# Layer 0's cross-attention by halves of eight tiles, with block transposes on VectorE and row-tiled sums on TensorE

## The chip, the core and the metric

One core of a Trainium2 chip runs the whole computation in one launch. The metric is the device time of that launch in microseconds, the median of a few runs. TensorE multiplies matrices into PSUM (eight banks of 128 partitions x 512 fp32), VectorE and ScalarE work on PSUM and SBUF, GpSimd on SBUF, and SyncE issues most of the DMAs. All data are fp32.

## The reference

Two layers follow each other. Layer 0 has one head: 2048 states x of width 256 attend to 1601 context tokens of width 192, and a gate mixes the result into the state. Layer 1 has 16 heads of width 16: self-attention over the 2048 states, cross-attention over the context, and an MLP. The change is in layer 0, whose reference is:

```python
tok = input_tokens @ W_proj + b_proj
scores = jnp.einsum('bnd,bsd->bns', prev_states, tok) / jnp.sqrt(jnp.float32(D))
attn = jax.nn.softmax(scores, axis=-1)
routed = jnp.einsum('bns,bsd->bnd', attn, tok)
ps_n = _ln(prev_states, g_state, beta_state)
in_n = _ln(routed, g_input, beta_input)
...
return _ln(new_state, g_out, beta_out)
```

Both kernels never form tok. They project the query instead (y = x W_proj^T, so that a score is y times the context token, plus x times b_proj), sum the context tokens under the probabilities (the mean context, width 192), and project that mean by W_proj.

## The kernel before

The 2048 states are 16 tiles of 128. The context lies transposed in two buffers: ctxA holds its first 128 features, ctxB the last 64, twice, on partitions 0 to 63 and 64 to 127. `queries` (L233) makes y for 512 states at a time. For a tile, `scores_a` (L252) multiplies the 128 features and `scores_b` (L266) the 64 features, key pieces alternating between the two copies of ctxB, which use different 64-row groups of the array; the scores of 1601 keys fill one PSUM tile of four banks, of which there is one. `scores_b` also forms the bias x times b_proj (L279, L281), takes the maximum (L283 to L285) and the exponential with its sum (L288), and the sum's reciprocal (L292).

`l0_values` (L321) transposes the probabilities on TensorE, 13 blocks of up to 128 keys (L327), copies them out of PSUM (L331, L333, L336), multiplies them by the context with keys on partitions (`ctxn`, L339, 13 matmuls of 192 columns), and scales by the reciprocal (L347). `l0_turn` (L350) transposes that mean context (2 transposes, L353, and a copy, L357); `l0_project` (L360) multiplies by W_proj (L362), adds b_proj (L365) and takes the statistics of the result and of x (`norm_stats`, L148: L150 and L151).

The loop at L404 runs these functions one tile apart: scores of tile t, the turn and projection of tile t-2, the values of tile t-1. Within layer 0 nothing is pinned: a scheduler places the instructions of each engine by priority and readiness. After tiles 6, 10 and 14, `begin_in` (L373) starts the inverse roots of the variances for four tiles (`inverse_root`, L153: two steps on VectorE, twelve on GpSimd, L166 to L169, then `ms` on VectorE, L379), and `normed_tile` and `routed_tile` normalize four tiles (L388, L394). Loads stand on SyncE's queue in the order of L92 to L207, the weights of the gate and of layer 1 among them.

`l0.close()` (L420) frees the PSUM banks, and all later work takes its banks from a new pool of eight. From there on every instruction is pinned in program order (`kept`, `mm` at L432, `transpose` at L435). What comes first is written out by hand as a list of steps, FIRST (L1018: ti are transposes of the normalized inputs, u, r, c the gate's matmuls, bi the inverse roots, nx and nr normalizations, and so on); then the attention of layer 1 runs from about 405 us, its 32 x 128 score matmuls on four row groups at once.

Of the kernel before, what the change touches and what calls it, by code (L numbers as in the profile page):

```python
# [70 lines left out]
def xattn_kernel(  # L71
# [19 lines left out]
    w_proj_sb = pa.tile([CK, 2, D], F32, name="w_proj_sb")  # L91
    nc.sync.dma_start(w_proj_sb, w_proj.rearrange("(c p) n -> p c n", p=CK))  # L92
    xT_sb = pa.tile([P, 2, S], F32, name="xT_sb")

    def load_xT(b):
        at_b = slice(b * QB, (b + 1) * QB)
        nc.sync.dma_start(xT_sb[:, :, at_b], xT.rearrange("(c p) n -> p c n", p=P)[:, :, at_b])
# [3 lines left out]

    ctxA = pa.tile([P, L], F32, name="ctxA")
    nc.sync.dma_start(ctxA, ctxT[:P])
    ctxB = pa.tile([P, L], F32, name="ctxB")
# [3 lines left out]
    nc.scalar.dma_start(cols_sb, cols)  # L108

# [24 lines left out]
    def load_compact(pool, w, p, name, queue=nc.gpsimd):  # L134

        k, n = w.shape
        stage = w_prep.tile([p, k // p, n], F32, name="stage")
        queue.dma_start(stage, w.rearrange("(c p) n -> p c n", p=p))
        t = pool.tile([p, k // p, D], F32, name=name)
        for c in range(k // p):  # L140
            nc.gpsimd.tensor_copy(
                t[:, c, :].rearrange("p (h w) -> p h w", w=HD),
                stage[:, c, :].rearrange("p (h w) -> p h w", w=HP)[:, :, :HD],
            )
        return t


    def norm_stats(mv, src, t):  # L148
        st = small.tile([P, 6], F32, name="bn_st", bufs=4)
        nc.vector.bn_stats(st, src)  # L150
        nc.vector.bn_aggr(mv[:, t, :], st)  # L151

    def inverse_root(var, name, n=4, bufs=2, keep=None):  # L153


        keep = keep or kept
        v, y, a = (small.tile([P, n], F32, name=f"{name}_{x}", bufs=bufs) for x in "vya")
        i32 = mybir.dt.int32
        keep(nc.vector.tensor_scalar_add(v, var, EPS))
        keep(  # L160
# [4 lines left out]
        for _ in range(3):  # L165
            keep(nc.gpsimd.tensor_mul(a, y, y))  # L166
            keep(nc.gpsimd.tensor_mul(a, a, v))
            keep(nc.gpsimd.tensor_scalar(a, a, -0.5, 1.5, ALU.mult, ALU.add))
            keep(nc.gpsimd.tensor_mul(y, y, a))  # L169
# [12 lines left out]
    pw = l0.enter_context(tc.tile_pool(name="pw", bufs=2, side="right"))  # L182
    y_sb = pa.tile([P, 2, S], F32, name="y_sb")
    ctxn = pa.tile([P, len(LC), C], F32, name="ctxn")
# [8 lines left out]
    nc.sync.dma_start(l0_rows, rows[:first_rows].partition_broadcast(P))  # L193
    load_x(0)
    load_xT(1)
    load_xT(2)
    load_xT(3)
    for t4 in range(1, 4):
        load_x(t4)
    w_u_sb = load_weights(p0, w_u, P, "w_u_sb", nc.sync)  # L200
    w_r_sb = load_weights(p0, w_r, P, "w_r_sb", nc.sync)
    w_n_sb = load_weights(p0, w_n, P, "w_n_sb", nc.sync)
    nc.sync.dma_start(rows_sb, rows[first_rows:].partition_broadcast(P))
    sa_wk_sb = load_compact(w_prep, sa_wk, P, "sa_wk_sb", nc.sync)
    sa_wv_sb = load_compact(w_prep, sa_wv, P, "sa_wv_sb", nc.sync)
    ca_wk_sb = load_compact(w_prep, ca_wk, CK, "ca_wk_sb", nc.sync)
    ca_wv_sb = load_compact(w_prep, ca_wv, CK, "ca_wv_sb", nc.sync)  # L207

    ps_s = l0.enter_context(tc.tile_pool(name="ps_s", bufs=1, space=PSUM))
    ps = tc.alloc_tile_pool(name="ps_tok", bufs=4, space=PSUM)  # L210

    warm = pa.tile([P, QB], F32, name="warm")
    nc.vector.memset(warm, 0.0)
    pt = ps.tile([P, QB], F32, name="tok_ps")
    for _ in range(3):
        nc.tensor.matmul(pt, warm[:, :P], warm, start=True, stop=True)


    wT_sb = pa.tile([P, 2, D], F32, name="wT_sb")
    pt = ps.tile([P, QB], F32, name="tok_ps")  # L220
    for d in range(2):
        for c in range(2):
            nc.tensor.transpose(
                pt[:, d * C + c * CK : d * C + (c + 1) * CK],
                w_proj_sb[:, c, d * P : (d + 1) * P],
                ident[:CK, :CK],
            )
    wT = pt[:, : 2 * C].rearrange("p (d n) -> p d n", d=2)
    nc.vector.tensor_copy(wT_sb[:, :, :C], wT)
    nc.scalar.copy(wT_sb[:, :, C:], wT[:, :, P:])  # L230


    def queries(b):  # L233
        for m in range(2):
            pt = ps.tile([P, QB], F32, name="tok_ps")
            for c in range(2):
                nc.tensor.matmul(  # L237
                    pt,
                    wT_sb[:, c, m * P : (m + 1) * P],
                    xT_sb[:, c, b * QB : (b + 1) * QB],  # L240
# [3 lines left out]
            copy = nc.vector.tensor_copy if m else nc.scalar.copy  # L244
            copy(y_sb[:, m, b * QB : (b + 1) * QB], pt)
# [3 lines left out]
    LEFT = 2 * QB - (L + 1) // 2  # L249
    KEYS = [(0, QB - LEFT), (QB - LEFT, QB), (2 * QB - LEFT, QB), (3 * QB - LEFT, L - 3 * QB + LEFT)]  # L250

    def scores_a(t):  # L252

        sc = ps_s.tile([P, 4 * QB], F32, name="l0_sc")[:, LEFT : LEFT + L]
        for n0, nw in KEYS:
            nc.tensor.matmul(  # L256
                sc[:, n0 : n0 + nw],
                y_sb[:, 0, t * P : (t + 1) * P],
                ctxA[:, n0 : n0 + nw],
# [928 lines left out]
```

## Time and profile before

| what | us |
|---|---|
| median of 3 runs (1946.67 to 1948.96) | 1947.11 |
| the profiled execution, its own time | 1949.57 |
| its span, first to last instruction | 1947.8 |
| outside the span | 1.8 |
| layer 0, up to layer 1's first transposes | 217.0 |
| FIRST, up to the attention loop | 188.0 |
| attention and MLP, to the end | 1542 |
| mean granted TensorE clock | 0.998 |

Over the span TensorE is busy 99% of the time, VectorE 73%, ScalarE 69%, GpSimd 34%. These are averages over stages that differ, so a stage is read from a window: its length, then for each engine the busy time with the count of instructions in brackets, the granted clock, the DMA share and the rate. The chain of waits is followed back from the last instruction; read forward it gives start, duration, engine and line. A group of instructions gives busy time, mean length of one in ns, idle time of its engine ahead of them, and what ended most of that idle time.

### The profile page before, as it was taken

What the parts mean: (1) busy time and instruction counts of PE and PEld (TensorE: products, weight loads), DVE (VectorE), ACT (ScalarE), POOL (GpSimd) and SP (SyncE); (2) the same over time, 40 slices, a digit from 0 to 9 for tenths busy, and PEclk for the clock granted to TensorE, in tenths of its full rate; (3) what the DMA queues carried; (4) which work ended last, traced back from release to release, by engine and by line L of the source; (5) the groups of instructions that cost most, each with busy time, mean ns of one, the idle gap of its engine ahead of it and who ended that gap; (6) DMA issues with size and microseconds to landing.
All of it is one profiled execution on the core that took longest, in us unless ns stands there. A gap on an engine that the chain in (4) does not pass through costs nothing.

```text
span 1947.8 us, 37207 instructions
## 1 busy us (share of the span) xinstructions
PE 1932.9 (99%) x13800; PEld 884.6 (45%) x13800; DVE 1425.3 (73%) x2617; ACT 1342.0 (69%) x2555; POOL 657.9 (34%) x833
## 2 busy tenths in 40 slices
PE   8999999999999999999999999999999999999999
PEld 4778776533333333443333334433333433443366
DVE  3444477778888888888888888788888878886210
ACT  2322433268887888788878887887888788888621
POOL 0100324124443444344344444343544344443010
PEclk9999999999999999999999999999999999999999
DMA  7000402600000000000000000000000000000000
GB/s 227 12 1 1 60 1 56 82 14 5 5 5 5 5 5 5 5 5 8 5 5 5 5 5 5 5 5 4 26 27 5 6 6 5 5 5 2 1 22 22
DMA packets 25605, 33.15 MB, mean 17 GB/s; under 512 B 11984, under 2 KB 17808, under 8 KB 25040
## 3 DMA queue, kind: packets, MB, share of 16 engines
q1 hardware_dynamic: 23200, 24.21, 5.7%
q0 software_dynamic: 1568, 4.90, 0.9%
q10 hardware_dynamic: 656, 1.67, 0.6%
q8 instruction: 108, 1.77, 0.4%
q14 instruction: 73, 0.60, 0.1%
HBM read 16.21 MB, written 2.62 MB: 10 GB/s over the span
## 4 chain that ended last, share of the span: by engine, by line
PE 93%; DVE 5%; POOL 1%; DMA 1%; issue 0%; ACT 0%; SPq 0%; DVEq 0%; ACTq 0%
PE bank L432 82%; PE l_rp L339 3%; PE l_sc L256 2%; DVE mxp L585 2%; PE l_sc L270 1%; PE l_tp L327 1%; PE bank L435 1%; PE l_rp L362 1%; DMA xT_sb<-in_xT_dram 1%; PE tok_ps L237 1%; DVE bn_st L807 0%; DVE bn_st L742 0%; DVE res L908 0%; PE l_rp L353 0%; POOL ca_wo_sb L451 0%
## 5 line engine op out<-in xcount | busy, mean ns | idle before, releaser
L585 DVE TENSOR_REDUCE mxp<-bank 128x1 f32<-128x512 f32 x1792 | 1109.0, 681 | 176.7 <-PE bank L432 170.3
L631 ACT ACTIVATE pt<-bank 128x512 f32<-128x512 f32 (+1 forms) x1856 | 960.2, 603 | 202.7 <-PE bank L432 201.2
L657 POOL TENSOR_TENSOR acc<-acc,part 128x512 f32<-128x512 f32 x414 | 525.1, 1268 | 841.4 <-ACT part L656 841.4
L432 PE MATMUL bank<-qa,k_sa 32*128 32x512 f32 x2048 | 520.0, 615 | 0.4
L432 PE MATMUL bank<-k_sa,qa 32*128 32x512 f32 x2048 | 507.1, 618 | 1.3 <-DVE mxp L585 0.8
L432 PE MATMUL bank<-k_ca,qa 32*128 32x512 f32 (+1 forms) x2048 | 432.9, 532 | 0.0
L432 PE MATMUL bank<-qa,k_ca 32*128 32x512 f32 (+1 forms) x1664 | 414.7, 617 | 0.0
L432 PEld LDWEIGHTS bank<-qa,k_sa 32*128 32x128 f32 x2048 | 215.8, 183 | 226.0 <-DVE mxp L585 203.5
L432 PE MATMUL bank<-pt,v_sa 128*32 128x512 f32 x2048 | 272.8, 605 | 0.4
L656 ACT COPY part<-bank 128x512 f32<-128x512 f32 x414 | 253.0, 611 | 13.5 <-PE bank L432 10.8
L432 PEld LDWEIGHTS bank<-qa,k_ca 32*128 32x128 f32 (+1 forms) x1664 | 166.3, 179 | 179.2 <-DVE mxp L585 143.4
L432 PEld LDWEIGHTS bank<-k_sa,qa 32*128 32x128 f32 x2048 | 199.4, 183 | 71.9 <-ACT pt L631 42.9
L432 PE MATMUL bank<-pt,v_ca 128*32 128x512 f32 (+1 forms) x1664 | 225.0, 605 | 0.3
L432 PEld LDWEIGHTS bank<-k_ca,qa 32*128 32x128 f32 x2048 | 196.9, 184 | 46.6 <-ACT pt L631 31.5
L432 PEld LDWEIGHTS bank<-pt,v_sa 128*32 128x32 f32 x2048 | 40.3, 108 | 192.7 <-ACT pt L631 191.7
L432 PEld LDWEIGHTS bank<-pt,v_ca 128*32 128x32 f32 (+1 forms) x1664 | 34.6, 108 | 151.1 <-ACT pt L631 149.0
L1106 DVE TENSOR_TENSOR o<-bank,res 128x512 f32<-128x512 f32 (+1 forms) x9 | 5.6, 630 | 97.1 <-PE bank L432 97.1
L339 PE MATMUL l_rp<-ctxn,l_pT 128*128 128x192 f32 (+1 forms) x416 | 70.4, 326 | 0.3 <-DVE routed L365 0.3
L283 DVE TENSOR_REDUCE l_nmx<-l_sc 128x1 f32<-128x1601 f32 x16 | 29.2, 1825 | 56.6 <-PE l_sc L270 56.6
L339 PEld LDWEIGHTS l_rp<-ctxn,l_pT 128*128 128x128 f32 (+1 forms) x416 | 67.2, 190 | 0.5 <-DVE routed L365 0.5
L357 ACT COPY l_uT<-l_rp 96x256 f32<-96x256 f32 x16 | 5.9, 367 | 73.9 <-PE l_rp L353 73.9
L432 PE MATMUL bank<-hT_sa,k_sa 128*128 128x512 f32 x128 | 55.7, 593 | 0.0
(189 smaller groups left out, 1393.4 us busy)
## 6 DMA issues: line engine op xcount, KB each, us to landing
xT_sb<-in_xT_dram SPq DMA_DIRECT2D x4, 512.0 KB
res<-in_x_dram SPq DMA_DIRECT2D x4, 512.0 KB
k_sa<-hT_sa SPq DMA_DIRECT2D x16, 128.0 KB
k_sa<-k SPq DMA_DIRECT2D x64, 32.0 KB
qa<-hT_sa SPq DMA_DIRECT2D x64, 32.0 KB
qa<-hT SPq DMA_DIRECT2D x64, 32.0 KB
k_sa<-in_mlp_w_dram POOLq DMA_DIRECT2D x2, 1024.0 KB, 6.1
out_dram<-o SPq DMA_DIRECT2D x7, 256.0 KB
```

Of the source, the lines that this page charges most:

```text
L237: nc.tensor.matmul(pt, wT_sb[:, c, m * P : (m + 1) * P], xT_sb[:, c, b * QB : (b + 1) * QB], start=(c == 0), stop=(c == 1),)
L256: nc.tensor.matmul(sc[:, n0 : n0 + nw], y_sb[:, 0, t * P : (t + 1) * P], ctxA[:, n0 : n0 + nw], start=True, stop=False, skip_group_check=True,
L270: nc.tensor.matmul(sc[:, n0 : n0 + nw], y_sb[r, 1, t * P : (t + 1) * P], ctxB[r, n0 : n0 + nw], start=False, stop=True, skip_group_check=True,
L283: nc.vector.tensor_reduce(nmx, sc, AX.X, ALU.max, negate=True)
L327: nc.tensor.transpose(tp[:kw, i, :], pr[:, k0 : k0 + kw], ident)
L339: nc.tensor.matmul(rp[:, :C], pT[:kw, i, :], ctxn[:kw, i, :], start=(i == 0), stop=(i == len(LC) - 1),)
L362: nc.tensor.matmul(rp[:, :D], uT[:, c, :], w_proj_sb[:, c, :], start=(c == 0), stop=(c == 1))
L432: kept(nc.tensor.matmul(out_, lhsT, rhs, **kw))
L585: kept(nc.vector.tensor_reduce(mxps[n][:, j, qt, kb : kb + 1], mx, AX.X, ALU.max))
L631: kept(nc.scalar.activation(pt[:kw], sc[:kw], AF.Exp, scale=HD**-0.5))
L656: kept(nc.scalar.copy(part, av))
L657: kept(nc.gpsimd.tensor_add(accs[n], accs[n], part))
```

## The change

Layer 0 is rewritten and pinned in program order.

- **PSUM.** One pool of four halves of two banks serves everything in layer 0, in rotation. Scores of a tile take two halves (801 and 800 keys); maximum and exponential run once per half.
- **Bias.** x times b_proj runs on GpSimd, its sum on ScalarE.
- **Transposes.** The probabilities (1601 keys filled up to 1632) are transposed by one VectorE instruction per tile in 32 x 32 blocks, into a buffer that holds eight tiles: on row group i (32 partitions) stand the keys of a block against the states 32i to 32i+31 of each tile.
- **Context.** TensorE transposes the context as before; then 20 SBUF-to-SBUF DMAs on SyncE's queue (16, and 4 for the last key) put each block of 32 keys on all four row groups (ctx4). Their source lies where the transposed probabilities of tiles 6 and 7 go later. The last two loads of x stand behind them.
- **Mean context.** For eight tiles at a time: 51 key blocks x 4 row groups, each a matmul of 32 x 128 with 256 columns (8 tiles x 32 states), and the same for the other 64 features, where key blocks alternate between the two column halves of the array. The four accumulators are all four halves. The result is already transposed; eight copies put it over y's buffer (alternating halves of the 64 features are summed by W_proj's lower part being there twice).
- **Projection.** Eight matmuls of 256 columns for four tiles into one half; the reciprocal and b_proj are applied by one VectorE instruction per tile, with the statistics behind it.
- **Order.** Scores of tiles 0 to 7, the first mean, scores of tiles 8 to 15, projection and inverse roots of the first eight tiles, the second mean, projection of the rest. The statistics of x stand ahead of the first mean. The gate's weights are loaded over the context's buffer after tile 15, and the row constants after them; layer 1's weights pass one by one through one staging buffer. FIRST loses the steps that moved into layer 0 (nx1, bi0, bi1) and gets bi2 and bi3.

```diff
@@ loads and buffers @@
-    w_proj_sb = pa.tile([CK, 2, D], F32, name="w_proj_sb")
-    xT_sb = pa.tile([P, 2, S], F32, name="xT_sb")
-    ctxA = pa.tile([P, L], F32, name="ctxA")
+    w_projA = pa.tile([P, D], F32, name="w_projA")
+    w_projB = pa.tile([P, D], F32, name="w_projB")
+    xy_sb = pa.tile([P, 2, S], F32, name="xy_sb")
+    ctx_w = p0.tile([P, 2 * L], F32, name="ctx_w")
+    ctxA, ctxB = ctx_w[:, :L], ctx_w[:, L:]
...
+    pr_xn = p0.tile([P, 2, LP], F32, name="pr_xn")
+    pT = pa.tile([P, T8, LP], F32, name="l0_pT")
+    ctx4 = pa.tile([P, KB, C], F32, name="ctx4")
+    wT_sb = rows_sb[:, : 2 * D].rearrange("p (d n) -> p d n", d=2)
+    xbs = [rows_sb[:, (2 + i) * D : (3 + i) * D] for i in range(2)]
+    stage = rows_sb[:, 4 * D : 8 * D]
...
-    ps_s = l0.enter_context(tc.tile_pool(name="ps_s", bufs=1, space=PSUM))
-    ps = tc.alloc_tile_pool(name="ps_tok", bufs=4, space=PSUM)
+    halves = l0.enter_context(tc.tile_pool(name="halves", bufs=4, space=PSUM))
+    def half():
+        return halves.tile([P, 2, QB], F32, name="half")
...
@@ scores_a, scores_b, l0_values, l0_turn, l0_project become @@
+    def query_bias(t):
+
+        xb = xbs[t % 2]
+        kept(nc.gpsimd.tensor_mul(xb, res[:, t, :], row("b_proj")))
+        kept(nc.scalar.activation(xb, xb, AF.Identity, accum_out=cbs[:, t : t + 1]))
...
+    def scores(t):
+        hs = [half().rearrange("p b n -> p (b n)") for _ in range(2)]
+        pieces = [hs[0][:, LEFT:], hs[1][:, : L - H0]]
+        outs = [pieces[i // 2][:, n0 - (i // 2) * H0 :][:, :nw] for i, (n0, nw) in enumerate(KEYS)]
+        tok = slice(t * P, (t + 1) * P)
+
+
+        for o, (n0, nw) in zip(outs, KEYS):
+            mm(
+                o, xy_sb[:, 0, tok], ctxA[:, n0 : n0 + nw],
+                start=True, stop=False, skip_group_check=True,
+            )
+        for i, (o, (n0, nw)) in enumerate(zip(outs, KEYS)):
+            r = slice(i % 2 * (C - P), (i % 2 + 1) * (C - P))
+            mm(
+                o, xy_sb[r, 1, tok], ctxB[r, n0 : n0 + nw],
+                start=False, stop=True, skip_group_check=True,
+            )
+        nm2 = small.tile([P, 2], F32, name="l0_nm2")
+        for i in range(2):
+            kept(nc.vector.tensor_reduce(nm2[:, i : i + 1], pieces[i], AX.X, ALU.max, negate=True))
+        nmx = small.tile([P, 1], F32, name="l0_nmx")
+        cb = cbs[:, t : t + 1]
+        kept(
+            nc.vector.scalar_tensor_tensor(
+                nmx, nm2[:, 0:1], nm2[:, 1:2], cb, ALU.min, ALU.subtract
+            )
+        )
+        kept(nc.vector.tensor_scalar(nmx, nmx, cb, 1.0 / 16.0, ALU.add, ALU.mult))
+        for i, (k0, kw) in enumerate(((0, H0), (H0, L - H0))):
+            kept(
+                nc.scalar.activation(
+                    pr_xn[:, t % 2, k0 : k0 + kw], pieces[i], AF.Exp, bias=nmx, scale=1.0 / 16.0,
+                    accum_out=dens[:, t, i : i + 1],
+                )
+            )
+
+    def turned(t):
+        kept(nc.vector.transpose(pT[:, t % T8, :], pr_xn[:, t % 2, :]))
...
+    def spread_context():
+        for j in range(P // HP):
+            r = slice(j * HP, (j + 1) * HP)
+            n = (KB - 1 - j) // 4 + 1 if j != (KB - 1) % 4 else (KB - 1) // 4
+            for i in range(P // HP):
+                nc.sync.dma_start(ctx4[i * HP : (i + 1) * HP, j::4, :][:, :n, :], tok_ctx[r, :n, :])
+        left = L - (KB - 1) * HP
...
+    def mean_context(h):
+
+
+        accs = [half() for _ in range(4)]
+
+        def part(dst, i, kb, feats, **kw):
+            r = slice(i * HP, (i + 1) * HP)
+            mm(
+                dst[:, : T8 * HP].rearrange("p (t a) -> p t a", a=HP),
+                ctx4[r, kb, feats],
+                pT[r, :, kb * HP : (kb + 1) * HP],
+                skip_group_check=True,
+                **kw,
+            )
+
+        for kb in range(KB):
+            for i, acc in enumerate(accs):
+                part(acc[:, 0, :], i, kb, slice(0, P), start=(kb == 0), stop=(kb == KB - 1))
+        for kb in range(KB):
+            c = slice(kb % 2 * (C - P), (kb % 2 + 1) * (C - P))
+            for i, acc in enumerate(accs):
+                part(acc[c, 1, :], i, kb, slice(P, C), start=(kb < 2), stop=(kb >= KB - 2))
...
+        for c in range(2):
+            for i, acc in enumerate(accs):
+                copy = nc.vector.tensor_copy if (i % 2 and c) else nc.scalar.copy
+                kept(
...
+    def project(t4):
+
+        pt = half().rearrange("p b (i d) -> p (b i) d", d=D)
+        for i in range(4):
+            tok = slice((4 * t4 + i) * P, (4 * t4 + i + 1) * P)
+            for c, w in enumerate((w_projA, w_projB)):
+                mm(pt[:, i, :], xy_sb[:, c, tok], w, start=(c == 0), stop=(c == 1))
+        return pt
+
+    def project_end(t4, pt):
+        for i in range(4):
+            t = 4 * t4 + i
+            kept(
+                nc.vector.scalar_tensor_tensor(
+                    routed[:, t, :], pt[:, i, :], rdens[:, t : t + 1], row("b_proj"),
+                    ALU.mult, ALU.add,
+                )
+            )
+            norm_stats(mv_r, routed[:, t, :], t)
...
@@ the order @@
-    pend, mean = (0, *got), None
-    for t in range(1, NT):
-        sc = scores_a(t)
-        if mean:
-            mean = l0_turn(*mean)
-        got = scores_b(t, sc)
-        if mean:
-            l0_project(*mean)
-        mean = l0_values(*pend)
-        pend = (t, *got)
-        if t in (6, 10, 14):
-            begin_in((t - 6) // 4, loose)
-        if 8 <= t < 12:
-            normed_tile(xn0[t - 8], t - 8, loose)
-            routed_tile(t - 8, loose)
-    l0_project(*l0_turn(*mean))
-    l0_project(*l0_turn(*l0_values(*pend)))
+    xns = {b: [pr_xn[:, b, i * D : (i + 1) * D] for i in range(4)] for b in range(2)}
+    xns.update({2: xns[0], 3: xns[1]})
+
+
+    queries(0)
+    query_bias(0)
+    scores(0)
+    turn_context(0, 4)
+    turn_context(4, 4)
+    query_bias(1)
+    scores(1)
+    turned(0)
+    turn_context(8, 4)
+    turn_context(12, 1)
+    spread_context()
+    for t4 in range(2, 4):
+        load_x(t4)
+    queries(1)
+    for t in range(2, T8):
+        query_bias(t)
+        scores(t)
+        turned(t - 1)
+    queries(2)
+    queries(3)
+    turned(T8 - 1)
+    for t in range(T8, NT):
+        query_bias(t)
+    sa_wk_sb = load_compact(w_prep, sa_wk, P, "sa_wk_sb", nc.sync, stage)
+    sa_wv_sb = load_compact(w_prep, sa_wv, P, "sa_wv_sb", nc.sync, stage)
+    wqs = {"sa": load_compact(w_prep, sa_wq, P, "sa_wq_sb", nc.sync, stage)}
+    ca_wk_sb = load_compact(w_prep, ca_wk, CK, "ca_wk_sb", nc.sync, stage)
+    ca_wv_sb = load_compact(w_prep, ca_wv, CK, "ca_wv_sb", nc.sync, stage)
+    for t in range(NT):
+        norm_stats(mv_x, res[:, t, :], t)
+    mean_context(0)
+    scores(T8)
+    for t in range(T8 + 1, NT):
+        scores(t)
+        turned(t - 1)
+
+    w_u_sb, w_r_sb, w_n_sb = (
+        ctx_w[:, i * 4 * D : (i + 1) * 4 * D].rearrange("p (c n) -> p c n", n=D) for i in range(3)
+    )
+    for t, w in ((w_u_sb, w_u), (w_r_sb, w_r), (w_n_sb, w_n)):
+        nc.sync.dma_start(t, w.rearrange("(c p) n -> p c n", p=P))
+    nc.sync.dma_start(rows_sb, rows[first_rows:].partition_broadcast(P))
+    got = [project(t4) for t4 in range(2)]
+    turned(NT - 1)
+    for t4 in range(2):
+        project_end(t4, got[t4])
+        begin_in(t4)
+    for b in range(2):
+        for i in range(4):
+            normed_tile(xns[b][i], 4 * b + i)
+    for t in range(4):
+        routed_tile(t)
+    mean_context(1)
+    got = [(t4, project(t4)) for t4 in range(2, 4)]
+    for t4, pt in got:
+        project_end(t4, pt)
     l0.close()
...
@@ FIRST @@
-        "nx1 ti0.2 ti0.3 ti0.0 ti0.1 ti1.0 bi3 nr2 nr1 ti1.1 u0.0 r0.0 r0.1 u0.1 nx2 c0.0 ti1.2 "
-        "b0.0 ti1.3 nr3 c0.1 b0.1 ro0 r1.0 ti2.0 r1.1 no0.0 ti2.1 u1.0 no0.1 no0.2 no0.3 ti2.2 "
+        "ti0.2 ti0.3 ti0.0 ti0.1 ti1.0 nr1 ti1.1 u0.0 r0.0 bi2 r0.1 u0.1 nx2 c0.0 bi3 ti1.2 "
+        "b0.0 ti1.3 nr2 c0.1 b0.1 nr3 ro0 r1.0 ti2.0 r1.1 no0.0 ti2.1 u1.0 no0.1 no0.2 no0.3 ti2.2 "
```

## The prediction

> **What bounds the kernel now.** I read the clock, the chain that ended last, the chain inside one tile of layer 0, and the windows by stage. The granted clock is 0.998, so durations are full-rate ones. The chain of the whole span, by engine:
>
> ```profile
> PE 93%; DVE 5%; POOL 1%; DMA 1%; issue 0%; ACT 0%; SPq 0%; DVEq 0%; ACTq 0%
> ```
>
> TensorE carries it. Layer 0 is the stretch up to 217 us, where layer 1's first transposes start. One tile of it, in the chain of waits:
>
> ```profile
> 47.84 2.69 PE l_sc L256 x8
> 50.54 0.22 PE l_rp L353 x2
> 50.76 1.54 PE l_sc L270 x8
> 52.30 1.06 PE l_rp L362 x4
> 53.36 1.44 PE l_tp L327 x13
> 54.80 4.25 PE l_rp L339 x26
> ```
>
> Nothing but TensorE: 11.2 us a tile, every one back to back. 4.23 are scores; 1.44 + 4.25 transpose probabilities and sum the context; 0.22 + 1.06 turn and project. The windows (a tile, the last tile, what follows layer 0):
>
> ```profile
> core 0: us, PE busy (x) PEld busy (x) DVE busy (x) ACT busy (x) POOL busy (x), PEclk, DMA share, GB/s
> 35.40:38.90 3.50, 3.50 (x7) 1.88 (x8) 0.56 (x1) 0.31 (x1) 0.73 (x2) 0.52 0.42 126
> 59.06:70.30 11.24, 11.24 (x62) 8.93 (x62) 5.22 (x14) 3.13 (x5) 0.00 (x0) 1.00 0.01 2
> 205.96:217.00 11.04, 9.18 (x53) 7.38 (x52) 3.30 (x11) 1.72 (x4) 0.46 (x1) 1.00 0.00 0
> 217.00:405.00 188.00, 186.20 (x779) 118.41 (x780) 131.75 (x291) 61.98 (x101) 54.68 (x170) 0.99 0.35 54
> 405.00:1947.00 1542.00, 1538.46 (x11978) 611.14 (x11976) 1202.24 (x2078) 1222.47 (x2361) 586.76 (x576) 1.00 0.03 7
> ```
>
> VectorE (5.22) and ScalarE (3.13) leave half of a tile free, so work can be moved to them. What TensorE saves before 217 us moves all that follows forward; the last two rows, 1730 us, are untouched but for a few reordered instructions.
>
> **The rates.** An fp32 matmul is two passes of the array, and the scores' first eight passes (2 x 1601 columns) take 2.69 us: 0.84 ns a column, 0.427 us for 512, 0.2135 for 256. Thirty-two-row tiles on four row groups run side by side: in layer 1, 16 passes of 512 columns take 1.93 us (1001.16 to 1003.09), 3.5 times faster than 16 x 0.427, and inside the burst four passes start every 0.429, so the full factor of 4 once running. Four 32-column tiles with 128 rows also run together (8 passes, L432 pt,v_sa, in about 1.0 us). Row and column tiles at once are not in the trace.
>
> **Scores.** TensorE does the same 2.69 + 1.54 = 4.23. What VectorE does per tile is interpolated from these groups:
>
> ```profile
> L585 DVE TENSOR_REDUCE mxp<-bank 128x1 f32<-128x512 f32 x1792 | 1109.0, 681 | 176.7 <-PE bank L432 170.3
> ...
> L339 PE MATMUL l_rp<-ctxn,l_pT 128*128 128x192 f32 (+1 forms) x416 | 70.4, 326 | 0.3 <-DVE routed L365 0.3
> L283 DVE TENSOR_REDUCE l_nmx<-l_sc 128x1 f32<-128x1601 f32 x16 | 29.2, 1825 | 56.6 <-PE l_sc L270 56.6
> ```
>
> The maximum in two halves: 1601 columns take 1.825 (L283), 512 take 0.681 (L585), so 801 take 0.985 each; two 128x1 operations 0.36 (L284, L285); the 32x32-block transpose of 1632 columns, from L615 (32 wide, 0.211) and L679 (512 wide, 0.700), 0.211 + 1600 x 1.02 ns = 1.84. Sum 4.17. That is as long as TensorE's 4.23; I take 4.27 a tile. If L679's rate fails at this width the cover is gone and each 0.1 us costs 1.6 in all. ScalarE: two halves of the exponential at 0.87 (L288: 1.597 for 1601) and a read of 0.19 each, 2.1, and the bias sum 0.6 in the first half: not late. The copies out of PSUM (L331, L333, L336: 0.93 on VectorE, 1.18 on ScalarE a tile) vanish; they were beside TensorE and bring nothing.
>
> **Start.** The new order has one PSUM pool of four two-bank halves. Scores of tile 1 need tile 0's: tile 0's exponential ended at 24.0 in the trace because x's rows landed late; I expect 20.7, as the loads are fewer and 1 comes before it. The second query block then waits for tile 1's exponential (27.7), and tile 2 starts at 31.2. Before, at 36.3, one tile was scored; now two are at 31.2. Six more at 4.27: 56.8. Two query blocks of 8 passes, 6.9, and their two copies, 1.4, whose halves the mean takes: **65.1**. The SBUF-to-SBUF copies that put the context on all row groups (20 DMAs, 4.9 MB, 768-byte rows) run beside this; they must land before the transpose of tile 6 overwrites their source. The 16-partition copies k_sa<-hT_sa moved 105 to 139 GB/s; the 1 KB rows of the loads 340. So 15 to 47 us. The new DMAs read 32 partitions; I take twice the nearest row, 23 us, from 30 to about 55. Needed at 58: hidden, with 3 us to spare. Behind them on SP's queue stand the last two loads of x (needed after tile 7) and the five layer-1 weights, which pass one by one through a single buffer with GpSimd's copies; all have the first mean to land in. The 16 statistics of x, 0.57 each (L150, L151), 9 us of VectorE, lie beside the first mean too.
>
> **Mean context, per half.** 204 matmuls of 32x128 and 256 columns, 408 passes of 0.2135: 87.1 us serial. Over four row groups 21.8 at the full factor, 24.9 at 3.5; the long run is nearer to the steady starts, so 22.5. The second 204 take 64 columns and alternate column halves: 10.9 if eight tiles run together, 21.8 if four; the nearest row (four column tiles at once) has them together, but issue must keep up with a weight load and a pass every 27 ns, where the densest stretch I find (900.02 to 900.53) has 51 ns. I take 13.5: **36 us**, between 33 and 47. It replaces 8 x 5.7 = 45.6 (L327, L339). The moving operand comes in 8 runs of 32 columns; the trace shows no such stride: I bound it by nothing and 10%, and take nothing, as every row there goes by its count of columns.
>
> The burst above shows 3.5 times, 4 once running. The Trainium skill, page "TensorE: Matmul & The Clock Gate", Part 3 ("Measured speedup vs the span model"), speaks against this step: four row tiles are given 3.07 times there, nine row-and-column tiles 6.32. An estimate by that page makes the parts 28.4 and 15.5 us, 8 a half more, and the time about 1951; the trace's own rows decide here.
>
> **From there.** Mean ends at 101.1; copies 0.9; 8 tiles 34.2: 136.2. Projection of 8 tiles, 16 matmuls of 256 columns at 0.43: 6.9 (before, 16 x 1.28 with its turns): 143.1.
>
> **The new wait.** The second mean takes all four halves; two of them hold the projection. They come free when VectorE has finished both projection ends, and its queue holds ahead of the second: the maxima of tile 15 and, behind ScalarE's exponentials, its transpose (2 x 0.985 + 0.36 + 2 x 0.87 + 1.84: 5.9 after 136.2), four ends of the first at 1.0 (L365 0.43, L150 0.43, L151 0.18), the first inverse root, whose last step waits for GpSimd's 12 operations at 0.28 (L166 to L169), 3.5 with its VectorE steps, then four more ends, 4.0 and two hand-overs of 0.1. 136.2 + 5.9 + 4.0 + 3.5 + 4.2 = 153.8: TensorE **stands for 10.7 us**. TensorE's longest stop in layer 0 of before, about 17.6 to 19.63, left the clock at 1.00; the row 35.40:38.90 has it at 0.52 for 3.5 us behind the context's transposes. After 10.7 us it holds (nothing) or falls like that (half of 3.5, with edges 2 us); I take 2.
>
> The same page, Part 1, states that the clock is halved after an idle window of some 3.4 us and given back after a busy one; the row's length fits, layer 0 of before shows no such stop, and the page's estimate would be 1.7 us of loss.
>
> Second mean: 153.8 + 2 + 36 = 191.8; copies 1.0, projection 6.9: 199.7. Layer 1's pool needs all of PSUM, so its first transpose waits for the last projection end, eight of them at 0.43 to 1.0 beside and behind the projection: 4.1, **203.8**. Before: 217.0. Gain 13.2. Cross-check by TensorE's work: a tile goes from 11.22 to 4.27 + 4.5 + 0.87 = 9.64, 25 us over 16; the earlier start gives 5, and the wait, the clock, the copies and the tail take 17 back.
>
> **The rest.** The first normalizations of layer 1 move into layer 0: -0.5. Its own clock dips and later weight rows (w_u, w_r, w_n are loaded only after tile 15, 1.5 MB, 70 us ahead of use) +1.2. Profiled execution: 1949.57 - 13.2 - 0.5 + 1.2 = 1937.1; it stands 2.46 above the median of 1947.11, so the forecast is 1934.6, **1935**.
>
> **Rivals.** A (0.50): as above, 1925 to 1942 by mean 33 to 39 and the wait 7 to 12.
> E (0.15): eight tiles run fully together and the wait is shorter (the inverse root hides): 6 + 4 less, 1924 to 1930. For: column tiles together in L432.
> B (0.17): the second part runs only four wide, +8.3 a half (21.8 for 13.5): 1951.2; half of it within 0.2%, half slower. For: no 32-row tile of the trace shares its row group with another.
> D (0.08): the copies move at the 16-partition rate, 47 us: they end at 77, mean and tile 6 wait 6 to 18: 1941 to 1953. Against: twice as many partitions.
> C (0.10), the other side: TensorE cannot issue 32-row passes fast enough, and each costs 60 ns: 1632 passes are 98 us instead of 72, so 1961. It gets slower than before from 52 ns a pass on (72 + 12.5 us over 1632 passes); the densest stretch shown has 51. For: that stretch. Against: within a burst, starts are 7 ns apart.
> That the change shortens nothing, since the mean is not in fact packed, lies beyond C: serial, the mean alone would be 174 us a half where 45.6 are removed; I give it nothing, as the row groups are written out and the trace shows them at work.
>
> **Numbers.** Within 0.2% (3.9 us, about what a measurement can tell from no change) is 1943.2 to 1951.0. Faster: A, E and a little of D: 0.68; same: half of B and most of D: 0.14; slower: C and the rest: 0.18. The range leaves out C and the end of E: 1925 to 1954.
>
> **What would show it.** In the profile after: scores (matmuls on ctxA and ctxB) at 4.27 a tile (over 4.4 means VectorE sets the pace); two mean stretches of 36 us each, 22.5 and 13.5; one idle stretch of TensorE of about 10.7 before the second, ended by VectorE's projection end; the first transposes of layer 1 at 203.8; 188 us from there to the attention loop. Wrong if the second part is as long as the first, if the copies end after 58, or if a wait of similar length stands at the start of the first mean.

## The result and the profile after

Twenty runs of each kernel: 1944.16 us (median; 1939.86 to 1947.88) against 1948.20 (1946.43 to 1949.88). The ratio is 0.998, with a 95% interval of 0.9973 to 0.9987: 4.0 us are gained, where 12.5 were forecast. The profiled execution of the changed kernel took 1942.26 (span 1940.5), 1.9 below its median; that of the kernel before (1949.57) lies 1.4 above its median in these runs. So 3.3 of the 7.3 us by which the two traces differ belong to the choice of executions.

The chain that ended last, by engine, and the group of the row-tiled matmuls (busy us, mean ns; idle us ahead of them):

```profile
PE 82%; DVE 5%; POOL 1%; DMA 1%; issue 0%; SPq 0%; ACT 0%; ACTq 0%; DVEq 0%
...
L98 PE MATMUL half<-l_pT,ctx 32*128 32x256 f32 (+1 forms) x1632 | 73.0, 385 | 11.4 <-DVE routed L410 9.1
```

TensorE still carries the time, and 9.1 us of idle stand ahead of the row-tiled work, released by the projection's end on VectorE. The windows by stage: scores of tiles 2 to 7, first mean, scores of 8 to 15, stop (with the first six matmuls of the second mean, which wait in it), second mean, stop, and the opening of layer 1; then a stop inside layer 1 and what follows it, and the whole stretch from layer 1's start to the attention loop:

```profile
core 0: us, PE busy (x) PEld busy (x) DVE busy (x) ACT busy (x) POOL busy (x), PEclk, DMA share, GB/s
31.29:57.86 26.57, 26.57 (x98) 14.03 (x96) 20.99 (x26) 13.07 (x34) 3.62 (x5) 1.00 0.96 182
64.86:102.05 37.19, 34.88 (x817) 30.41 (x816) 6.93 (x29) 4.93 (x18) 7.81 (x16) 1.00 0.26 84
103.23:138.70 35.47, 35.47 (x128) 18.77 (x128) 28.04 (x38) 14.09 (x31) 0.00 (x0) 1.00 0.01 3
145.82:156.42 10.60, 1.53 (x7) 0.59 (x7) 6.97 (x25) 2.07 (x4) 4.68 (x24) 0.63 0.00 1
156.42:192.98 36.56, 36.56 (x810) 31.59 (x810) 4.04 (x15) 0.00 (x0) 4.96 (x24) 0.92 0.01 3
201.50:206.10 4.60, 0.05 (x1) 0.03 (x1) 4.29 (x14) 0.00 (x0) 4.43 (x7) 1.00 0.48 54
206.10:211.00 4.90, 4.90 (x27) 4.85 (x28) 0.50 (x2) 3.96 (x6) 4.21 (x11) 0.65 0.91 131
321.10:325.20 4.10, 1.50 (x6) 0.42 (x5) 2.67 (x7) 2.61 (x6) 2.86 (x8) 0.70 0.25 57
325.20:333.00 7.80, 7.80 (x20) 5.49 (x21) 7.47 (x17) 2.07 (x3) 1.26 (x2) 0.50 0.21 45
206.10:401.40 195.30, 190.16 (x780) 121.02 (x780) 130.28 (x290) 62.30 (x102) 55.47 (x186) 0.97 0.34 51
```

Read the clock, third figure from the right. It is 1.00 in the first mean and in the scores, and falls with the stops of TensorE that these rows show: in the stop from 145.8, into the second mean (0.92), at layer 1's first transposes (0.65), and from 322.8 to 333.0 us in layer 1, around a stop of 2.6 us. The kernel before has no such stop there, but a shorter dip all the same, 3.4 us long:

```profile
332.30:335.80 3.50, 3.50 (x14) 3.14 (x14) 3.43 (x8) 1.55 (x2) 0.00 (x0) 0.51 0.21 48
```

No idle of TensorE over 0.34 us stands in the 9 us ahead of that dip. So a stop is not the only thing that brings the half clock. Layer 1 begins at 206.1, not at 217.0: 10.9 us gained. From there to the end 1734.4 us pass, where it was 1730.8: 3.6 lost again, in code that the change hardly touches: 7.0 us are lost up to the first scores of layer 1 (their ninth pass starts 127.5 us after layer 1's start, before 120.6), and 3.4 won behind them.

### The profile page after: what moved, and what is told of

It is laid out like the page before. It is cut to its first block, busy times and chain, and to the rows that moved or that the text cites. A ratio compares the mean times of both kernels' runs of the same rounds, so it can differ in the third digit from the quotient of the medians.

```text
span 1940.5 us, 39176 instructions
## 1 busy us (share of the span) xinstructions
PE 1908.6 (98%) x14774; PEld 852.7 (44%) x14774; DVE 1430.3 (74%) x2554; ACT 1334.4 (69%) x2590; POOL 671.8 (35%) x850
## 4 chain that ended last, share of the span: by engine, by line
PE 82%; DVE 5%; POOL 1%; DMA 1%; issue 0%; SPq 0%; ACT 0%; ACTq 0%; DVEq 0%
PE bank L98 81%; DVE mxp L660 2%; PE bank L101 1%; DMA k_sa<-k 1%; DVE bn_st L882 0%; SPq L576 0%; DVE res L964 0%; DVE cand_sb L963 0%; DVE res L981 0%; DVE cand_sb L946 0%; DVE bn_st L817 0%; DVE cand_sb L962 0%; PE half L98 0%; DVE res L976 0%; DVE routed L410 0%
## 5 line engine op out<-in xcount | busy, mean ns | idle before, releaser
L98 PE MATMUL half<-l_pT,ctx 32*128 32x256 f32 (+1 forms) x1632 | 73.0, 385 | 11.4 <-DVE routed L410 9.1
L98 PE MATMUL half<-ctx_w,xy_sb 128*128 128x512 f32 (+5 forms) x256 | 71.1, 516 | 1.9 <-DVE xy_sb L388 1.2
L98 PEld LDWEIGHTS half<-l_pT,ctx 32*128 32x128 f32 (+1 forms) x1632 | 62.6, 163 | 21.9 <-DVE routed L410 10.0
L313 ACT ACTIVATE pr_xn<-half,l_nmx 128x801 f32<-128x801 f32 (+1 forms) x32 | 29.4, 925 | 44.2 <-DVE l_nmx L310 44.2
```

Source lines behind the costliest of these rows:

```text
L98: kept(nc.tensor.matmul(out_, lhsT, rhs, **kw))
L313: nc.scalar.activation(pr_xn[:, t % 2, k0 : k0 + kw], pieces[i], AF.Exp, bias=nmx, scale=1.0 / 16.0, accum_out=dens[:, t, i : i + 1],)
```

## The experiments

The changes of time are against the changed kernel's median, 1944.2; each run was timed beside the kernel before (1947.3 to 1947.8). Gains of 1.6 and 2.5 us are not clear of noise by the medians alone: the ratios of those runs to the kernel before (0.9974, 0.9967 and 0.9973) have intervals that overlap the changed kernel's 0.9973 to 0.9987. There the traces have to show what moved.

**Order between the halves.**

```diff
     for t4 in range(2):
         project_end(t4, got[t4])
+    for t4 in range(2):
+        project_stats(t4)
         begin_in(t4)
```

(`project_end` now holds the scaling alone, `project_stats` the statistics.)

> One edit of the changed kernel: between the halves VectorE first runs all eight projection ends, then the statistics and the inverse roots; the end of layer 0 is left as it was. Theory 1 (TensorE's stop ahead of the second mean, and the half clock behind it, cost what VectorE's order makes them cost): the stop that lasted from 146 to 156.4 us ends about 148.4 (tile 15's transpose at 144.7 and eight ends at 0.44), no half clock follows since the stop is 2 to 3 us, the second mean takes 33.5 instead of 36.8: layer 1 begins about 195, 11 us earlier than 206.1; time about 1933. Rival (the gain is lost later whatever layer 0 does, because layer 1's first scores wait for copies on SyncE's queue): layer 1 begins 11 us earlier but the time moves by less than 5, to 1939 or more.

Measured: 1934.71, 9.5 us less. The stop shrinks to 2 us (counted, like the 10.6, from the mean's first matmul, 150.57 to 152.61), and the second mean runs at full clock:

```profile
150.57:186.32 35.75, 34.88 (x817) 30.96 (x816) 10.17 (x40) 2.07 (x4) 9.59 (x48) 1.00 0.01 3
```

That window runs from the first matmul, stop included; before it was 145.82 to 192.98, 47.2 us. Layer 1 begins at 199.4, not 195, because this execution started its first mean at 69.8 instead of 64.9 (see the start, below). The rival is out: what was gained here reached the end.

**Order at the end of layer 0.** The same split for the last eight tiles:

```diff
     for t4, pt in got:
         project_end(t4, pt)
+    for t4, pt in got:
+        project_stats(t4)
     l0.close()
```

> One edit of the changed kernel: at the end of layer 0 the eight projection ends run ahead of the statistics, so that PSUM is free sooner; the order between the halves is left as it was. Theory 1: layer 1's first transpose comes about 202.3 instead of 206.1 (3.8 us), the stop before it shrinks from 4.6 to under 1, and the half clock from 206.3 to 210.1, 1.9 us, goes with it: 5.7 in all, time about 1938.5. Rival (that dip belongs to the 24 transposes which open layer 1, not to the stop): the dip stays, and 3.8 us are gained, about 1940.4.

Measured: 1939.65, 4.5 us less. TensorE's stop ahead of layer 1 goes from 4.55 to 1.84 us, and the clock of the opening transposes is whole:

```profile
206.88:211.80 4.92, 4.84 (x32) 4.11 (x33) 3.82 (x16) 4.21 (x7) 4.91 (x11) 1.00 0.78 94
```

The same 24 transposes are there, so the dip (0.65 above) belonged to the stop, not to them. The stop was expected under 1 us: VectorE still had four ends to run behind the last projection (205.07 to 206.73).

**The query weights' load, moved in the list of steps.**

```diff
-        "no3.3 ts2.0 cw ts2.1 cv1 cv2 v1.2 L k2.0 v1.3 L ck0.1 rs3 q1 cv3 cv4 L ck1.1 cv5 cv6 ns3 "
-        "L cv7 L ck1.2 cv8 cv9 L ck0.2 ts3.0 L v2.0
+        "no3.3 ts2.0 ts2.1 cv1 cv2 v1.2 L k2.0 v1.3 L ck0.1 rs3 q1 cv3 cv4 L ck1.1 cv5 cv6 ns3 "
+        "L cv7 L ck1.2 cv8 cv9 L cw ck0.2 ts3.0 L v2.0
...
```

> One edit of the changed kernel: the step that loads the cross-attention's query weights (0.5 MB) and output weights stands 21 steps later in the hand-written list, behind the first scores of layer 1. Theory 2 (that load, which the change moved from 226 us to 308 us, runs beside the copies of the keys and holds them up): the first scores begin 112 us after layer 1's start instead of 114.7, the half clock at 322 to 332 us lasts 3.5 us as before, and the time falls by 2 to 4 us to about 1941. Rival (the copies are late because layer 0 ends earlier and the context's own load, 1.2 MB, lies beside them): nothing moves, 1944.

Measured: 1944.49. This tells nothing of the load: the scheduler put the load and its copies back where they were, and the order of the instructions on VectorE, ScalarE, GpSimd and SyncE is the changed kernel's. It is a second measurement of the changed kernel, and a useful one: 11 runs, 1943.0 to 1945.6, and a profiled execution that differs at the start from the first one.

**The row constants' load.** The changed kernel's scheduler had run this load ahead of the weights that stand before it, from 89 us on.

```diff
-        nc.sync.dma_start(t, w.rearrange("(c p) n -> p c n", p=P))
-    nc.sync.dma_start(rows_sb, rows[first_rows:].partition_broadcast(P))
+        kept(nc.sync.dma_start(t, w.rearrange("(c p) n -> p c n", p=P)))
+    kept(nc.sync.dma_start(rows_sb, rows[first_rows:].partition_broadcast(P)))
```

> One edit of the changed kernel: the 1.2 MB load of row constants stays behind the gate's weights on SyncE's queue, so it runs after tile 15 instead of during the first mean. Theory 3 (TensorE stood from 95.1 to 97.0 us in the first mean because its 16 KB instruction fetch, issued every 3.5 us there, queued behind that load): both gaps (1.9 and 0.7 us) vanish, the first mean takes 34.6 instead of 37.2, time about 1941.6. Rival (the gap belongs to the packed stream itself): the gap stays where it is, at the same point of the second part, 1944.

Measured: 1942.61, 1.6 less; in the trace the first mean takes 34.89, not 37.20, and both gaps are gone: 2.3 us. In the changed kernel the second part of the two means read like this:

```profile
88.30:102.05 13.75, 11.97 (x409) 9.32 (x408) 0.00 (x0) 0.00 (x0) 0.74 (x2) 1.00 0.24 88
181.53:192.98 11.45, 11.45 (x409) 9.60 (x408) 0.00 (x0) 0.00 (x0) 0.00 (x0) 1.00 0.02 4
```

The first one has DMA traffic beside it, the second has not. In the trace the packets of the instruction queue, 16 KB each, come 3.5 us apart there; the one due about 91.2 came at 94.8, at the end of the 1.2 MB load (issued at 89.2, its packets from 90.6 to 94.8 us), and TensorE went on at 96.9.

**The query weights' load, issued earlier.** In the changed kernel GpSimd's row of instructions and what waited (us in total, times, longest):

```profile
311.09 0.24 POOL L187 TENSOR_SCALAR rs_o_a<-rs_o_a 128x4 f32<-128x4 f32 x1
315.31 0.40 POOL L160 COPY ca_wq_sb<-stage 128x256 f32<-128x256 f32 x1 [3.98 <-DMA stage<-in_ca_wq_dram]
```

```profile
DVE ms_sa L888 <- POOL rs_sa_y L188: 10.9, 1, 10.9
ACT hn L997 <- DVE ms_sa L888: 8.0, 1, 8.0
...
PE bank L98 <- ACT k L1018: 2.6, 1, 2.6
```

GpSimd stands 4 us for a load, in the middle of an inverse root, with a second root queued behind it. VectorE, then ScalarE, then TensorE wait for that root. In the kernel before, the load was issued 90 us ahead of its use; its rows, before and after:

```profile
L138 POOL DMA_DIRECT2D stage<-in_ca_wq_dram x1: 741/741/741, 226.1 to 226.1; - x1
```

```profile
L156 POOL DMA_DIRECT2D stage<-in_ca_wq_dram x1: 792/792/792, 308.0 to 308.0; - x1
```

The old staging buffer lived from the start; the new one is a tile of a pool that opens only when layer 0's memory is given back. The edit (`load_compact` then copies without loading):

```diff
             nc.gpsimd.dma_start(ca["ctx"][:, c, :], ctxT[c * CK : (c + 1) * CK, :])
+        ca["wq"] = pc.tile([P, 4 * D], F32, name="stage")
+        kept(
+            nc.gpsimd.dma_start(
+                ca["wq"].rearrange("p (c n) -> p c n", c=2), ca_wq.rearrange("(c p) n -> p c n", p=P)
+            )
+        )
```

> One edit of the changed kernel: the load of the cross-attention's query weights is issued right behind the context's load (before GpSimd's memsets), and the scheduler then puts GpSimd's copies of it behind the inverse roots. Theory 2b (in the changed kernel GpSimd stood 4.0 us at 311.3 for that load, with two inverse roots queued behind it; ScalarE's normalization and TensorE waited for those): the eighth pass of layer 1's first scores comes 121 to 123 us after layer 1's start instead of 127.5, the half clock there is 3.5 us long instead of 10, and since the attention loop gives part of it back the time falls by 2 to 4 us, to 1940.5 to 1942.5. Rival (the keys' copies, sharing the DMA queues with the context's load, set it): no change within 1, 1944.

Measured: 1937.21, 7.0 less, more than expected; but the six runs spread from 1933.8 to 1941.7, and the profiled one is the slowest. Between the traces 5.9 us are gained: from layer 1's start to the end 1728.5 us pass instead of 1734.4. The pass that the expectation calls the eighth (the ninth in order of time) starts 121.6 us after layer 1's start (127.5 in the changed kernel, 120.6 before), and VectorE's wait is down:

```profile
DVE ms_sa L889 <- POOL rs_sa_y L189: 6.2, 1, 6.2
ACT hn L998 <- DVE ms_sa L889: 3.3, 1, 3.3
```

GpSimd's two copies (0.4 us each) now stand behind the roots, so this run does not part the wait for the load from the place of the copies; the wait was 4.0 us. I had thought that the attention loop gives half of such a delay back, since 7.0 us at the first scores had become 3.6 at the end. It does not: with the delay gone, the end comes 2.3 us sooner after layer 1's start than before. The loop itself is shorter in every execution of the changed layout (over 1528 passes of the first score product, from 512 on, 915.0 us, before 917.4). The difference comes in eleven steps of 0.16 to 0.26 us spread over the loop. Why is open; no run was made for it.

**Work in the stop.**

```diff
         accs = [half() for _ in range(4)]
+        if h:
+            for _ in range(20):
+                mm(accs[0][:, 0, :D], w_projA[:, :P], w_projA, start=True, stop=True, skip_group_check=True)
```

> The changed kernel with 20 extra matmuls of 128x128x256 (8.6 us) on TensorE in the stop ahead of the second mean; they write an accumulator that the mean then starts afresh. The stop itself is as long as before. Theory 1 in its clock half (TensorE's stop of 10 us brings the clock to 0.5 until 162): no dip there, the second mean runs at full rate from 156.4 on, 3.2 us gained, about 1941. Rival (the slow start of the second mean is its own, pipeline and instruction fetch): nothing gained, 1944.

Measured: 1941.70, 2.5 less. The stretch of the stop, now filled, and the second mean behind it:

```profile
148.45:159.14 10.69, 9.44 (x48) 7.72 (x46) 7.05 (x26) 2.07 (x4) 4.69 (x24) 1.00 0.00 1
159.14:192.80 33.66, 33.66 (x810) 30.38 (x810) 4.03 (x15) 0.00 (x0) 4.96 (x24) 1.00 0.01 3
```

From the stop's end the second mean takes 33.66 instead of 36.56 us, and the stretch is as long as the stop was. The clock alone is worth 2.9 us in the trace.

**Work among the first transposes.**

```diff
     def turn_context(i0, n, busy=0):
         pt = half()
+        for _ in range(busy):
+            mm(pt[:, 0, :], ctxA[:, :P], ctxA[:, :QB], start=True, stop=True, skip_group_check=True)
```

(`busy` is 1 in the second and the fourth group of transposes.)

> The changed kernel with two extra matmuls of 512 columns (0.86 us each) among the 26 transposes of the context at the start, so that no stretch of transposes and waiting is longer than 2.7 us. Theory 4 (the spread of the changed kernel, 1939.9 to 1947.9, comes from half-clock dips at 21 and 32 us, which some executions have and others have not, behind 3.7 and 3.3 us of transposes and waiting): the first mean begins at 66 us at most, without dips before it, the runs lie closer together (within 4 us) and the median falls by 1 to 2.5 to about 1942. Rival (the two dips are there for another reason, the start of the program): dips and spread stay, and the median rises by the 0.9 to 1.7 us of added work.

Measured: 1942.61, 1.6 less; eight runs, 1939.8 to 1943.5. The same stretch here, up to the first mean, and in the second execution of the changed kernel (the run whose list of steps was edited without effect):

```profile
16.00:66.00 50.00, 50.00 (x174) 25.35 (x172) 34.22 (x45) 23.45 (x60) 6.82 (x10) 1.00 0.71 164
```

```profile
16.00:69.00 53.00, 52.12 (x175) 26.50 (x173) 33.86 (x43) 23.23 (x59) 7.18 (x10) 0.97 0.68 157
```

The first mean begins at 65.7 and 69.2. Over the executions seen here that keep the old start, it begins between 64.6 and 70.2, with none, one or several dips ahead of it. This run can't decide for the theory, because the first trace of the changed kernel has no dip there either. The spread begins earlier, at the first product of the program. Here are its eight passes in the changed kernel's first trace, and in that of the kernel with the query weights' load issued earlier:

```profile
7.58 3.67 PE L98 MATMUL half<-xy_sb,rows_sb 128*128 128x512 f32 x8 [1.80 <-DMA xy_sb<-in_xT_dram]
```

```profile
8.45 6.42 PE L98 MATMUL half<-xy_sb,rows_sb 128*128 128x512 f32 x8 [2.35 <-DMA xy_sb<-in_xT_dram]
```

The passes start 0.43 us apart in the first and 0.85 in the second, as at half the clock. Four of the twelve profiles of the changed layout are like the first: their first scores begin at 11.7 to 12.0 us, their first mean at 64.6 to 66.4, and none has a dip between 21 and 35 us (two of them with the added matmuls, two without). In the other eight the first scores begin at 13.6 to 15.5 and the first mean at 66.4 to 70.2; all seven without added matmuls have such dips, and the one with them (the last run below) has none. So the added matmuls may help where the start is late, but one profile carries that, and a dip at 8 to 13 us, ahead of all these transposes, they can't touch.

**Shapes in the scores.**

```diff
+        b_first = t % 2 == 1
+        for part in ("BA" if b_first else "AB"):
+            first = part == ("B" if b_first else "A")
+            for i, (o, (n0, nw)) in enumerate(zip(outs, KEYS)):
+                r = slice(i % 2 * (C - P), (i % 2 + 1) * (C - P))
+                lhsT, rhs = (xy_sb[:, 0, tok], ctxA) if part == "A" else (xy_sb[r, 1, tok], ctxB[r])
+                mm(
+                    o, lhsT, rhs[:, n0 : n0 + nw],
+                    start=first, stop=not first, skip_group_check=True,
+                )
```

> One edit of the changed kernel: tiles with odd numbers multiply their 64-row features first and their 128-row features last, so that TensorE changes between the two shapes once a tile instead of twice. Theory 5 (the scores' pitch of 4.44 us instead of the forecast's 4.27 is the change of shape: each costs 0.2 us, in which no weights are loaded ahead): pitch 4.23 to 4.25, 14 tiles, 2.5 to 2.9 us gained, about 1941.5. Rival (VectorE sets the pitch): pitch stays over 4.35, under 1 us gained.

Measured: 1940.33, 3.9 less. The pitch in the trace is 4.24 us for 4.44 in 11 of 12 steady intervals, so 2.8 us are shown; the other 1.1 is within what executions differ. So a change between 128-row and 64-row tiles costs 0.2 us, and VectorE did not set the pitch. The two products alone, at 0.834 ns a column (0.427 over 512), are 2.67 + 1.33 = 4.0, which with two changes makes 4.4 of the 4.44.

**Column halves.**

```diff
-            c = slice(kb % 2 * (C - P), (kb % 2 + 1) * (C - P))
+            hc = kb // 26
+            c = slice(hc * (C - P), (hc + 1) * (C - P))
             for i, acc in enumerate(accs):
-                part(acc[c, 1, :], i, kb, slice(P, C), start=(kb < 2), stop=(kb >= KB - 2))
+                part(acc[c, 1, :], i, kb, slice(P, C), start=(kb in (0, 26)), stop=(kb in (25, KB - 1)))
```

> One edit of the changed kernel: in the mean context's second part the key blocks take one column half for the first 26 blocks and the other for the last 25, instead of alternating, so that only four tiles are at work at a time. Theory (alternation is what let eight tiles run at once, at 27.0 ns a pass): 53 to 54 ns a pass, the second part 21.8 instead of 11.2 us, both halves together 21 to 22 us, time about 1965. Rival (27 ns comes from the weights being half as wide, not from two tiles in one row group): 27 to 35 ns a pass, time 1944 to 1950.

Measured: 1961.88, 17.7 more, and slower than before (ratio 1.0067, 1.0054 to 1.0080). The second part takes

```profile
93.34:114.80 21.46, 21.46 (x409) 15.04 (x408) 0.00 (x0) 0.00 (x0) 0.47 (x2) 1.00 0.17 57
```

54.0 ns a pass instead of 27.0. Without the alternation the whole change would have been a loss. The gaps of the first mean are not in this trace, though the load of the row constants (issued at 93.8 us) still runs beside it: at this rate the instruction packets come 7 us apart.

**All edits**, without and with the scores' new order.

> All edits that the theories ask for in one: projection ends first at both places, the row constants after tile 15, the query weights' load earlier, the two matmuls among the transposes. If the theories add up: 10 us (order between the halves, measured 9.5 to 10), 4.5 (order at the end), 1.6 (row constants), 2 to 4 (query weights), 1 to 2.5 (start): 19 to 22 us below the changed kernel, 1922 to 1925. Rival (they overlap, since each removes one half-clock dip that another would have had anyway): 1928 to 1931.

> The kernel with all edits (1921.4) and, besides, the odd tiles' scores in the other order of the two shapes. If theory 5 holds there too: 2.5 to 2.9 us less, 1918.5 to 1919. Rival (VectorE is the bound of the scores): 1921.

Measured: 1921.35 (1920.3 to 1922.2) and 1918.55 (1917.8 to 1919.4); against the kernel before 0.9864 (0.9851 to 0.9877) and 0.9849 (0.9835 to 0.9862). The first five edits add up (9.5 + 4.5 + 1.6 + 7.0 + 1.6 = 24.2; together 22.8), so hardly any of them took what another would have given. The last one, 2.8 us less, agrees with the 0.2 us a change of shape. The two means of the first of these kernels, the second with its stop of 2 us:

```profile
66.36:101.25 34.89, 34.36 (x817) 30.70 (x816) 6.94 (x29) 4.93 (x18) 7.82 (x16) 1.00 0.18 56
145.01:180.70 35.69, 34.81 (x817) 30.95 (x816) 10.16 (x40) 2.07 (x4) 9.68 (x48) 1.00 0.04 16
```

Its layer 1 begins at 191.1, and of the dips after the first mean one is left, at 307 to 310 us, where the kernel before had its own.

## Why the prediction was too high, step by step

- **Start.** Forecast 65.1 for the first mean, traced 64.86; but its first passes wait for the query blocks' copies, and it gets going at 66.1. That this is so close is luck: the changed kernel's other execution has 69.2, and one trace was not enough to see that the start varies. The copies of the context took 27 us where 23 were forecast and ended at 58.0, 2 us ahead of the transpose of tile 6.
- **Mean context.** The packing was right, and better than taken: 54.0 ns a pass in the first part (four tiles, the full factor) and 27.0 in the second (eight tiles), 33.7 us a half undisturbed, where 36 was taken. TensorE issued a weight load and a pass every 27 ns, so rival C is out, and B too, though its mechanism, forced, costs 17.7 us. Of E the packing came true and the shorter wait did not. The Trainium skill, page "TensorE: Matmul & The Clock Gate", Part 3, gives 3.07 times for four row tiles; here the serial time of 213.5 ns a pass over 54.0 is 3.95. In the first mean 2.3 us of gaps took that gain back: the instruction fetch, which the prediction did not have.
- **Scores.** 4.44 a tile, not 4.27: 2.3 us over 14 tiles. The sum of 2.69 and 1.54 was taken from a chain in which other work stood between the two products; the changes of shape were not counted. VectorE, which was feared to be the bound, was not.
- **The new wait.** Forecast 10.7, traced 10.6, for the reason given. The clock behind it cost 2.9 instead of 2. A second dip, behind the stop at layer 0's end, cost 1.7; the forecast had 1.2 for all of layer 1's dips and later weight rows. Part 1 of the same page states that an idle window of some 3.4 us halves the clock and that this window runs freely. The stops of 4.5 us and more agree with it, and so does it that the same kernel shows different dips in different executions; the dip of the kernel before at 332.3, with no idle over 0.34 us ahead of it, does not follow from that rule. The page's Part 4 says that transposes do not count as work for the clock in the same way as other products. The traces here are divided on it: of nine profiles that have the context's transposes without added matmuls, seven have dips at 21 to 35 us and two have none, and the 24 transposes that open layer 1 ran at full clock behind the shorter stop (1.84 us).
- **Layer 0 as a whole.** It ended at 206.1, forecast 203.8. Errors of both signs stand in this: the scores and the instruction fetch cost 2.3 each more than forecast, the two means otherwise 2.3 and 1.4 less, and small steps 1.4 more.
- **The rest: here the prediction failed.** "The last two rows, 1730 us, are untouched but for a few reordered instructions", -0.5 and +1.2; traced, they are 3.6 longer. What mattered is a line of the change that the diff ahead of the prediction leaves out: `load_compact` for the cross-attention's query weights takes its staging buffer from a pool that opens at 303 us. The step counted the loads that the change moves within layer 0 and missed the one that it moves in layer 1, with GpSimd's copies behind it. With that load earlier 5.9 us go in the trace (7.0 between the medians), nearly half of the forecast gain. The rest of the 7.0 lost at layer 1's first scores goes with the dip behind the stop ahead of it: with all edits their ninth pass comes 120.6 us after layer 1's start, as before. It was luck that only 3.6 of it show at the end: what follows came out 3.4 shorter, 2.4 of it in the loop, which was not forecast and which no run explains.
- **From trace to median.** The forecast took the 2.46 us by which the profiled execution of before stood above its median and carried them over to the changed kernel. That kernel's profiled execution, with its early start, stands 1.9 below its median. This makes 4.4 us of the 9.6 between 1934.6 and 1944.2.

So the forecast 12.5 became 7.3 in the two traces (2.3 lost in layer 0, 2.9 more in layer 1 than was allowed for) and 4.0 between the medians.

## What to carry to other kernels

Where a change takes a buffer away, ask of every load that used it when it can now be issued, and what stands on the engine's queue behind the copy that waits for it. Let what frees PSUM run ahead of what only follows from it: the same VectorE work in another order was worth 9.5 and 4.5 us. The stops of TensorE of 4.5 us and more cost their length and a dip of the clock behind them (2.9 us behind the longest), so such a stop that can't be removed is worth filling. And one profiled execution does not give the distance between trace and median for another kernel.

## What the runs showed of the hardware that was not expected

- Tiles of 32 rows and 64 columns ran eight at a time, 27.0 ns for a weight load and a pass of 256 columns, with alternating column halves; 54.0 without.
- At that rate TensorE took 16 KB of instructions every 3.5 us, and a 1.2 MB load beside it held one fetch up: no pass started for 1.9 us.
- Changing between 128-row and 64-row tiles costs 0.2 us each time.
- The stop of 4.5 us ahead of layer 1 went with the half clock in all nine profiles that have it, the stop of 1.84 us in none of three. The stop of 10 us ahead of the second mean did in all eight that have it unfilled. Each of these dips, and each other recorded one before the program's end, was 3.4 us long, or two to four times that. Dips without a stop over 1.3 us are there too (the kernel before at 332 us, the one with all edits at 307).
